# Second attention of a group as one task on four banks, with two of its minima on VectorE

## The chip, the cores and the metric

The kernel runs on one core of one Trainium2 chip. The metric is the device time of that core in microseconds (us). TensorE does the matrix products, ScalarE and VectorE empty its PSUM banks and do the elementwise work, GpSimd (POOL in the profile) does elementwise work between SBUF tiles, and SyncE starts most transfers.

## The reference

The reference is one layer of a graph attention network over 128 batches of 64 nodes with 512 features, in fp32. Cut to what matters here:

```python
def gat_heads(x, adj, W, a):                     # W: [H, F, O]
    Wh = einsum('bnf,hfo->bhno', x, W)
    e = f1(Wh)[..., None] + f2(Wh)[..., None, :]
    e = where(e > 0, e, 0.01 * e)
    e = where(adj > 0, e, -1e9)
    return einsum('bhnm,bhmo->bhno', softmax(e), Wh)

h   = relu(layernorm(x))
h   = elu(gat_heads(h, adj, W_heads, a_heads))   # first attention, 4 heads of 512
out = elu(gat_heads(concat(h), adj, W_out, a_out))  # second attention, one head of 512
y   = relu(out @ w1 + b1) @ w2 + b2 + out
return x + layernorm(y) * gamma + beta
```

The elu is `x` for positive `x` and `exp(x) - 1` otherwise.

## The kernel before

The 8192 rows are 64 tiles of 128 rows; a group is 4 tiles, and there are 16 groups. Large products of 512x512 blocks are done by a scheme of seven products instead of eight (`unit`): each of the seven is one set of 4 matmul instructions of 256 columns per weight piece, each of which the trace records as two passes, so 8 records. The seven products use three PSUM banks, and several accumulate on a bank that another engine has changed or read in between:

```python
def unit(name, product, post, order):
    own = {1: 1, 2: 1, 5: 5, 3: 5, 6: 6, 7: 6, 4: 6}      # product -> its bank
    def after(p):
        if p in (1, 5, 6):
            nm = {1: "s1", 5: "s5", 6: "t"}[p]
            sb[nm] = wk.tile([P, 2, T], FP, tag=nm, name=f"{nm}_{name}")
            if p == 6:
                nc.vector.tensor_tensor(gb[6], gb[6], sb["s1"], ALU.add)   # line 254
            nc.scalar.copy(sb[nm], gb[p])                                  # line 255
            post(nm, sb[nm])
        elif p == 2: post("c11", gb[1])
        elif p == 7: post("c22", gb[6], sb["s5"], gb[1])
        elif p == 3: post("c12", gb[5], sb["t"], gb[5])
        else:        post("c21", gb[6])
    # ... (cut: emits the parts in the given order, `after` with high priority)
```

So product 7 goes onto the bank of product 6 after the add of line 254 and the copy of line 255, and product 4 goes onto the same bank after `post("c22", ...)` has read it.

The products of the first layer run head by head in `project1` (bank names `g_a` in the trace). Each of the four results (quadrants c11, c12, c21, c22) gets an elu:

```python
def elu(dst, src, name):
    ex = wk.tile([P, 512], FP, tag="elu", name=f"ex{name}", bufs=3)
    nc.scalar.activation(ex, src, AF.Relu, scale=-1.0)                     # line 571
    nc.scalar.activation(ex, ex, AF.Exp, scale=-1.0)                       # line 572
    nc.vector.scalar_tensor_tensor(dst, ex, -1.0, src, ALU.add, ALU.max)   # line 573

# in project1, post() of a quadrant:
    if b is not None:
        nc.vector.tensor_tensor(to, a, b, ALU.add)                         # line 603 (c12, c22)
        a = to
    elu(flat(dst), flat(a), f"{what}_{g}_{h}")
# ... (cut)
    s = unit(..., (1, 5, 6, 2, 3, 7, 4))
    return [
        s[0], lambda: (s[1](), flush_late()), lambda: (s[2](), next_sums()), s[3], s[4],
        lambda: (s[5](), late.append(s[6])),
    ]
```

A head has six steps: products 1, 5, 6, 2, 3, 7. Product 4 (quadrant c21) comes late, behind product 5 of the next head; for the last head it comes behind the first part of the next stage (`project2`, bank names `g_b`).

Beside the 24 steps of the four heads run the side tasks of `stage_e`, the second attention of the group before. They are spread evenly over the steps:

```python
def attend2(g, q):
    if q == 0:
        tag = "out" if g < NG - 1 else "z11"
        OUT[g] = big.tile([P, G, FO], FP, tag=tag, name=f"o{g}")
    pa = [aux([P, FO], f"pa2_{g}_{q}_{b}") for b in range(NB)]     # aux: 2 banks
    for b in range(NB):                                            # NB = 2 batches in a tile
        rows = slice(b * N, (b + 1) * N)
        for c in range(2):
            nc.tensor.matmul(                                      # line 754, 64x64, 512 columns
                pa[b][c * N:(c + 1) * N], AT2[g][rows, 2 * q + c, rows],
                WH2[g][rows, 2 * q + c, :], start=True, stop=True, skip_group_check=True,
            )
    for b in range(NB):
        elu(OUT[g][:, 2 * q + b], pa[b], f"2_{g}_{q}_{b}")

def stage_e(g):
    gap = [lambda: None]
    score = [lambda j=j: scores2(g, j) for j in range(G)]
    attend = [lambda q=q: attend2(g, q) for q in range(2)]
    return (
        gap + score + [lambda: spread2(g)] + gap * 2 + [lambda: softmax2(g)] + gap * 5
        + [lambda: transpose_weights2(g)] + gap * 2 + attend[0:1] + gap * 2 + attend[1:2] + gap * 4
    )
```

`stage_e` runs for groups 0 to 14; the last group calls `attend2` itself, beside the feed-forward part of group 14. Of the eight PSUM banks six are the main ring ("mm", used by `bank(...)`) and two are "aux". The first attention of the first group (`attend0`, bank names `pu`) already has an elu whose minimum is taken on VectorE: `tensor_scalar(ex, pa, 0.0, None, ALU.min)` and then one Exp on ScalarE, in place of Relu and Exp.

Of the kernel before, what the change touches and what calls it, by code (L numbers as in the profile page):

```python
# [9 lines left out]
FP = mybir.dt.float32  # L10
AF = mybir.ActivationFunctionType
ALU = mybir.AluOpType
# [10 lines left out]
def gat_preln_kernel(  # L23
# [30 lines left out]
    nc = tc.nc  # L54
    P = 128
# [3 lines left out]
    FO = W_out.shape[1]  # L59
    DF = w1.shape[1]  # L60
    NB = P // N
    KC = F // P
    NT = B * N // P
    G = 4
# [9 lines left out]
    big = ctx.enter_context(tc.tile_pool(name="big", bufs=1))  # L74
# [5 lines left out]
    def bank(name):  # L80
        return ps.tile([P, 2, T], FP, tag="mm", name=name)

    def flat(ap):
        return ap.rearrange("p a b -> p (a b)")
# [8 lines left out]
    def aux(shape, name):  # L93
        return ps.tile(shape, FP, tag="aux", name=name, bufs=2)
# [470 lines left out]

    H1, ZSUM = {}, {}

    def elu(dst, src, name):

        ex = wk.tile([P, 512], FP, tag="elu", name=f"ex{name}", bufs=3)  # L570
        nc.scalar.activation(ex, src, AF.Relu, scale=-1.0)  # L571
        nc.scalar.activation(ex, ex, AF.Exp, scale=-1.0)  # L572
        nc.vector.scalar_tensor_tensor(dst, ex, -1.0, src, ALU.add, ALU.max)  # L573

    def quadrant(what):
# [12 lines left out]
    def project1(g, h):  # L588
# [8 lines left out]
        def post(what, a, b=None, to=None):  # L597
            if what[0] != "c":
                return
            nm = {"c11": "11", "c12": "12", "c21": "S1", "c22": "22"}[what]  # L600
            dst = H1[nm][:, h]
            if b is not None:
                nc.vector.tensor_tensor(to, a, b, ALU.add)  # L603
                a = to
            elu(flat(dst), flat(a), f"{what}_{g}_{h}")
            if what == "c21":
                nc.gpsimd.tensor_tensor(dst, dst, H1["22"][:, h], ALU.add)  # L607
# [96 lines left out]
    A2, AT2, F2, OUT = {}, {}, {}, {}  # L704

    def scores2(g, j):
        if j == 0:
            F2[g] = sm.tile([P, 2, G], FP, tag="f2", name=f"f2_{g}")
        f = F2[g]
        for c in range(2):  # L710
            junk = wk.tile([P, FO], FP, tag="elu", name=f"jf{g}_{j}_{c}", bufs=3)
            nc.vector.scalar_tensor_tensor(  # L712
                junk, WH2[g][:, j], 1.0, ao[:, c, :], ALU.mult, ALU.mult,
                accum_out=f[:, c, j:j + 1],
            )

    def spread2(g):

        f = F2[g]
        dg = sm.tile([P, G, N], FP, tag="s2dg", name=f"s2dg{g}", bufs=1)  # L720
        nc.vector.tensor_tensor(
            dg, eye[:, None, :].to_broadcast([P, G, N]), f[:, 1][:, :, None].to_broadcast([P, G, N]),
            ALU.mult,
        )
        F2[g] = f, dg

    def softmax2(g):
        f, dg = F2.pop(g)
        pe = aux([P, G, N], f"s2pe{g}")
        nc.tensor.matmul(  # L730
            pe.rearrange("p h m -> p (h m)"), blkones.rearrange("p b n -> p (b n)"),
            dg.rearrange("p h m -> p (h m)"), start=True, stop=True,
        )
        A2[g] = softmax(pe, f[:, 0], G, "s2", g)

    def transpose_weights2(g):
        A = A2.pop(g)
        pt = aux([P, G, P], f"s2pt{g}")
        for j in range(G):
            nc.tensor.transpose(pt[:, j, :], A[:, j].rearrange("p b m -> p (b m)"), ident)  # L740
        AT2[g] = wk.tile([P, G, P], FP, tag="hT", name=f"at2_{g}", bufs=4)
        nc.scalar.copy(AT2[g], pt)

    def attend2(g, q):


        if q == 0:
            tag = "out" if g < NG - 1 else "z11"
            OUT[g] = big.tile([P, G, FO], FP, tag=tag, name=f"o{g}")
        pa = [aux([P, FO], f"pa2_{g}_{q}_{b}") for b in range(NB)]  # L750
        for b in range(NB):
            rows = slice(b * N, (b + 1) * N)
            for c in range(2):
                nc.tensor.matmul(
                    pa[b][c * N:(c + 1) * N], AT2[g][rows, 2 * q + c, rows],
                    WH2[g][rows, 2 * q + c, :], start=True, stop=True, skip_group_check=True,
                )
        for b in range(NB):
            elu(OUT[g][:, 2 * q + b], pa[b], f"2_{g}_{q}_{b}")

    def stage_e(g):

        gap = [lambda: None]
        score = [lambda j=j: scores2(g, j) for j in range(G)]
        attend = [lambda q=q: attend2(g, q) for q in range(2)]
        return (
            gap + score + [lambda: spread2(g)] + gap * 2 + [lambda: softmax2(g)] + gap * 5
            + [lambda: transpose_weights2(g)] + gap * 2 + attend[0:1] + gap * 2 + attend[1:2] + gap * 4
        )


# [173 lines left out]
    for g in range(NG):  # L945
        if g >= 1:
            side = stage_e(g - 1)
            done, n = 0, 6 * H
            for i in range(n):
                if i % 6 == 0:  # L950
                    steps = project1(g, i // 6)
                steps[i % 6]()
                while done * n < (i + 1) * len(side):
                    side[done]()
                    done += 1
            flush_late()
# [3 lines left out]
        if g == NG - 1:  # L960
            run(project2(g), tr + [nothing] * 6 + ff[:2])
            run(ff[2:], [
                lambda: [scores2(g, j) for j in range(G)], lambda: spread2(g), nothing, nothing,
                lambda: softmax2(g), *[nothing] * 7, lambda: transpose_weights2(g), nothing,
                *[lambda q=q: attend2(g, q) for q in range(2)], nothing,
            ])
            continue
# [67 lines left out]
```

## Time and profile before

| | |
|---|---|
| time, median of 3 runs | 2297.66 us (2297.63 to 2298.43) |
| VectorE busy | 1276.5 us (56%), 2227 instructions |
| ScalarE busy | 904.6 us (39%), 1633 instructions |
| GpSimd busy | 1019.9 us (44%) |
| weight loads (PEld) busy | 1891.7 us (82%), 11856 |
| TensorE clock granted | 0.999 |
| matmuls of the second attention (`pa`, 64x512) | 256 records, median 614 ns |
| Relu from `pa` on ScalarE | 64, median 592 ns |
| Exp of these elus | 64, median 630 ns |
| last instruction of these elus on VectorE | 64, median 684 ns |

PE is TensorE's matmul and PEld its weight load, which overlaps it; DVE is VectorE, ACT is ScalarE, POOL is GpSimd, SP is SyncE. [...] matmuls that follow each other overlap in the trace, and the distance from one start to the next says more than a duration. In the second attention four matmuls on four different 64x64 parts of the array start almost together.

### The profile page before, as it was taken

The numbers are of one execution on the slowest core, as the hardware profiler recorded it, in microseconds if no ns is written. First come the engines' busy times: TensorE is split into PE (matmuls) and PEld (weight loads), VectorE is DVE, ScalarE is ACT, GpSimd is POOL, SyncE is SP. The second block draws the span as 40 slices with busy tenths as digits, with TensorE's granted clock in tenths as the row PEclk, the third lists the DMA queues.
The fourth block names the chain that finished last, engine by engine and source line by source line (L and its number), as shares of the span: only waits on it lengthen the run. The fifth ranks groups of instructions, "written<-read, shape, count | busy, mean of one in ns | idle before, by whom it ended". The sixth has DMA issues, their size and how long they took to land. (4 is left out here: it accounts for less than half of the span.)

```text
span 2293.9 us, 33254 instructions
## 1 busy us (share of the span) xinstructions
PE 2273.2 (99%) x11856; PEld 1891.7 (82%) x11856; DVE 1276.5 (56%) x2227; ACT 904.6 (39%) x1633; POOL 1019.9 (44%) x906
## 2 busy tenths in 40 slices
PE   9999999999999999999999999999999999999997
PEld 4688888888888888888888888888888888888885
DVE  7554654755556555564655546555465554644427
ACT  3535244252542525335253352534425244251512
POOL 7653524444254442634425344353443525533324
PEclk9999999999999999999999999999999999999999
DMA  8554454544546445454544645445454454635543
GB/s 288 194 183 131 147 179 133 181 132 147 174 133 184 137 156 158 136 184 130 166 151 139 183 133 176 132 147 179 133 181 133 143 177 132 183 119 169 162 147 106
DMA packets 255012, 361.15 MB, mean 157 GB/s; under 512 B 23768, under 2 KB 143608, under 8 KB 254848
## 3 DMA queue, kind: packets, MB, share of 16 engines
q1 hardware_dynamic: 249568, 340.88, 47.6%
q0 software_dynamic: 4576, 16.81, 2.0%
q8 instruction: 96, 1.57, 0.3%
q10 hardware_dynamic: 704, 1.33, 0.2%
q14 instruction: 68, 0.56, 0.1%
HBM read 331.66 MB, written 27.26 MB: 156 GB/s over the span
## 5 line engine op out<-in xcount | busy, mean ns | idle before, releaser
L305 PE MATMUL g_b<-w,h 128*128 128x256 f32 x2560 | 593.2, 380 | 0.0
L305 PEld LDWEIGHTS g_b<-w,h 128*128 128x128 f32 x2560 | 481.5, 190 | 64.1 <-issue 2.0
L289 PE MATMUL g_a<-z,w 128*128 128x256 f32 x1440 | 341.8, 380 | 0.0
L289 PE MATMUL g_a<-zs_z,w 128*128 128x256 f32 x1440 | 336.0, 381 | 0.0
L289 PEld LDWEIGHTS g_a<-zs_z,w 128*128 128x128 f32 x1440 | 270.2, 190 | 59.0 <-issue 24.4
L289 PEld LDWEIGHTS g_a<-z,w 128*128 128x128 f32 x1440 | 272.5, 190 | 41.1 <-DVE g_a L603 5.0
L305 PE MATMUL g_b<-w,hS 128*128 128x256 f32 x1024 | 238.2, 379 | 0.0
L607 POOL TENSOR_TENSOR hS<-hS,h 128x512 f32<-128x512 f32 x60 | 78.0, 1300 | 359.7 <-DVE hS L573 359.7
L305 PEld LDWEIGHTS g_b<-w,hS 128*128 128x128 f32 x1024 | 192.2, 190 | 24.8 <-issue 0.2
L571 ACT ACTIVATE exc<-g_a 128x512 f32<-128x512 f32 x240 | 142.5, 594 | 163.9 <-DVE g_a L603 95.8
L573 DVE SCALAR_TENSOR_TENSOR h<-exc,g_a 128x512 f32<-128x512 f32 x180 | 123.6, 687 | 140.7 <-ACT exc L572 140.1
L572 ACT ACTIVATE exc<-exc 128x512 f32<-128x512 f32 x240 | 151.4, 631 | 6.6
L688 POOL TENSOR_TENSOR h<-h,h 128x512 f32<-128x512 f32 x64 | 86.8, 1364 | 138.7 <-PE g_b L305 138.7
L688 POOL TENSOR_TENSOR h<-hS,h 128x512 f32<-128x512 f32 x64 | 81.7, 1277 | 146.9 <-PE g_b L305 146.7
L314 POOL TENSOR_TENSOR zs_z<-zS,z 128x512 f32<-128x512 f32 x60 | 85.2, 1419 | 134.8 <-PE g_a L289 131.6
L489 ACT COPY at<-s1pt 128x512 f32<-128x512 f32 x64 | 34.4, 589 | 268.9 <-PE s1pt L485 268.9
L833 POOL TENSOR_TENSOR xr<-xr,bs 128x512 f32<-128x512 f32 x64 | 98.8, 1546 | 78.3 <-DMA xr<-in_x_dram 45.3
L305 PE MATMUL g_d<-w,rt 128*128 128x256 f32 x512 | 121.6, 380 | 2.2 <-DVE o L825 1.5
L289 PE MATMUL g_c<-ot,w 128*128 128x256 f32 x512 | 122.7, 383 | 0.6 <-DVE ot L792 0.6
L289 PE MATMUL g_a<-zS,w 128*128 128x256 f32 x480 | 113.4, 379 | 0.0
L305 PEld LDWEIGHTS g_d<-w,rt 128*128 128x128 f32 x512 | 97.0, 190 | 16.9 <-DVE o L825 2.7
L712 DVE SCALAR_TENSOR_TENSOR jf<-wh,ao 128x512 f32<-128x512 f32 x128 | 96.7, 792 | 24.1 <-ACT wh L694 23.8
(164 smaller groups left out, 3532.9 us busy)
## 6 DMA issues: line engine op xcount, KB each, us to landing
w<-tc SPq DMA_DIRECT2D x624, 256.0 KB, 2.7
w<-in_L_gnn_W_out_dram SPq DMA_DIRECT2D x192, 256.0 KB, 2.7
w<-in_L_gnn_W_heads_dram SPq DMA_DIRECT2D x180, 256.0 KB, 3.0
w<-in_L_gnn_w_dram SPq DMA_DIRECT2D x96, 256.0 KB, 2.7
x<-in_x_dram SPq DMA_DIRECT2D x64, 256.0 KB, 4.6
xr<-in_x_dram SPq DMA_DIRECT2D x128, 128.0 KB, 2.7
out_dram<-o SPq DMA_DIRECT2D x126, 128.0 KB, 2.4
tc<-pt POOLq DMA_DIRECT2D x20, 512.0 KB, 4.3
```

What stands on the lines that cost most here:

```text
L289: LAST["pe"] = nc.tensor.matmul(bk[:, o, :], w[:, k, ts(o, P)], a[:, k, :], start=start and o == 0 and k == 0, stop=k == 1, skip_group_che ...
L305: LAST["pe"] = nc.tensor.matmul(bk[:, j, :], a[:, k, ts(j, P)], w[:, k, :], start=start and n == 0, stop=i == len(ms) - 1 and k == 1, skip ...
L314: eng.tensor_tensor(s2, s1, a11, ALU.subtract)
L489: nc.scalar.copy(AT[t].rearrange("p b h n -> p (b h) n"), pt)
L571: nc.scalar.activation(ex, src, AF.Relu, scale=-1.0)
L572: nc.scalar.activation(ex, ex, AF.Exp, scale=-1.0)
L573: nc.vector.scalar_tensor_tensor(dst, ex, -1.0, src, ALU.add, ALU.max)
L607: nc.gpsimd.tensor_tensor(dst, dst, H1["22"][:, h], ALU.add)
L688: nc.gpsimd.tensor_tensor(dst[:, h], x0[:, h], x1[:, h], ALU.subtract)
L712: nc.vector.scalar_tensor_tensor(junk, WH2[g][:, j], 1.0, ao[:, c, :], ALU.mult, ALU.mult, accum_out=f[:, c, j:j + 1],)
L833: nc.gpsimd.tensor_tensor(xr, xr, bs, ALU.add)
```

## The change

The two attention tasks of a group (`q` 0 and 1, two banks each) become one task on four banks: the two aux banks and two of the main ring. All 8 matmul instructions stand together, and the four elus follow. It stands at step 19 of 24 (counted from 0), the second step of the last head; the two tasks before stood at steps 16 and 19. In each pair of elus the second takes its minimum on VectorE, as `attend0` does. The last group keeps two tasks but has the changed elus. It is for changing TensorE's tile size once instead of twice in a group, and for taking work off ScalarE where four elus follow each other.

```diff
-    def elu(dst, src, name):
+    def elu(dst, src, name, on_vector=False):
         ex = wk.tile([P, 512], FP, tag="elu", name=f"ex{name}", bufs=3)
-        nc.scalar.activation(ex, src, AF.Relu, scale=-1.0)
-        nc.scalar.activation(ex, ex, AF.Exp, scale=-1.0)
+        if on_vector:
+            nc.vector.tensor_scalar(ex, src, 0.0, None, ALU.min)
+            nc.scalar.activation(ex, ex, AF.Exp)
+        else:
+            nc.scalar.activation(ex, src, AF.Relu, scale=-1.0)
+            nc.scalar.activation(ex, ex, AF.Exp, scale=-1.0)
         nc.vector.scalar_tensor_tensor(dst, ex, -1.0, src, ALU.add, ALU.max)
 ...
-        pa = [aux([P, FO], f"pa2_{g}_{q}_{b}") for b in range(NB)]
+        second_attention(g, q, [aux([P, FO], f"pa2_{g}_{q}_{b}") for b in range(NB)])()
+
+    def attend2_all(g):
+        OUT[g] = big.tile([P, G, FO], FP, tag="out", name=f"o{g}")
+        pa = [[aux([P, FO], f"pa2_{g}_0_{b}") for b in range(NB)]]
+        pa.append([flat(bank(f"pa2_{g}_1_{b}")) for b in range(NB)])
+        for finish in [second_attention(g, q, pa[q]) for q in range(2)]:
+            finish()
+
+    def second_attention(g, q, pa):
         for b in range(NB):
 ...   (the matmuls as before)
-        for b in range(NB):
-            elu(OUT[g][:, 2 * q + b], pa[b], f"2_{g}_{q}_{b}")
+        def finish():
+            for b in range(NB):
+                elu(OUT[g][:, 2 * q + b], pa[b], f"2_{g}_{q}_{b}", b == 1)
+        return finish
 ...
-        attend = [lambda q=q: attend2(g, q) for q in range(2)]
         return (
             gap + score + [lambda: spread2(g)] + gap * 2 + [lambda: softmax2(g)] + gap * 5
-            + [lambda: transpose_weights2(g)] + gap * 2 + attend[0:1] + gap * 2 + attend[1:2] + gap * 4
+            + [lambda: transpose_weights2(g)] + gap * 4 + [lambda: attend2_all(g)] + gap * 4
         )
```

## The prediction

> **What bounds the kernel now.** I read the page's busy shares first, then the waits of TensorE and of its weight loads, then the timeline of one group, because the shares say which engine to look at and only the other two say whether it waits.
>
> ```profile
> span 2293.9 us, 33254 instructions
> PE 2273.2 (99%) x11856; PEld 1891.7 (82%) x11856; DVE 1276.5 (56%) x2227; ACT 904.6 (39%) x1633; POOL 1019.9 (44%) x906
> ```
>
> TensorE is busy for all but 20.7 us of the span. Busy is not speed, however, so the waits come next (columns: who waited for whom, us in total, times, longest).
>
> ```profile
> PE pab L177 <- DMA ar<-in_L_gnn_a_heads_dram: 4.5, 1, 4.5
> PE g_d L305 <- DVE o L825: 1.5, 1, 1.5
> ...
> PE pa L754 <- DVE o L573: 0.2, 1, 0.2
> ```
>
> All waits of matmuls on other engines and transfers add up to about 10 us, nearly all in the first and last stages. The weight loads show something else:
>
> ```profile
> PEld g_a L289 <- issue: 24.4, 30, 0.8
> ...
> PEld pa L754 <- issue: 5.3, 16, 0.3
> PEld pa L754 <- ACT exc L572: 5.0, 15, 0.3
> ...
> PEld g_a L289 <- DVE g_a L603: 5.0, 15, 0.3
> ```
>
> In the 15 groups with a side task there are two idle stretches per attention block that no other engine ends ("issue"): 0.33 us before its first load and 0.81 us before the first load of the next product. This is the array changing between 128x128 and 64x64 tiles. One more, of 0.33 us, comes 15 times and does have a releaser: a load of g_a that waits for VectorE at line 603. The timeline of one group shows both (start, us, engine, line; the groups repeat every 140.37 us to within 0.1 us):
>
> ```profile
> 335.52 0.21 PEld L754 LDWEIGHTS pa<-wh,at 64*64 64x64 f32 x8 [0.33 <-ACT exc L572]
> ...
> 336.54 1.59 PEld L289 LDWEIGHTS g_a<-zs_z,w 128*128 128x128 f32 x8 [0.81 <-issue]
> ...
> 338.15 1.70 PEld L289 LDWEIGHTS g_a<-z,w 128*128 128x128 f32 x8
> ...
> 343.64 0.21 PEld L754 LDWEIGHTS pa<-wh,at 64*64 64x64 f32 x8 [0.33 <-issue]
> ...
> 343.75 0.60 ACT L571 ACTIVATE exc<-g_a 128x512 f32<-128x512 f32 x1 [1.14 <-PE g_a L289]
> ...
> 344.66 1.59 PEld L289 LDWEIGHTS g_a<-zs_z,w 128*128 128x128 f32 x8 [0.81 <-issue]
> ...
> 345.04 0.69 DVE L573 SCALAR_TENSOR_TENSOR hS<-exc,g_a 128x512 f32<-128x512 f32 x1 [2.98 <-ACT exc L572]
> ...
> 347.33 0.69 DVE L573 SCALAR_TENSOR_TENSOR o<-ex,pa 128x512 f32<-128x512 f32 x1 [0.46 <-ACT ex L572]
> 347.94 0.69 DVE L254 TENSOR_TENSOR g_a<-g_a,s_a 128x512 f32<-128x512 f32 x1
> 348.00 3.43 PEld L289 LDWEIGHTS g_a<-zs_z,w 128*128 128x128 f32 x16
> ...
> 348.66 0.59 ACT L255 COPY t_a<-g_a 128x512 f32<-128x512 f32 x1 [1.36 <-DVE g_a L254]
> ...
> 351.46 0.84 PEld L305 LDWEIGHTS g_b<-w,h 128*128 128x128 f32 x4
> ...
> 351.87 0.70 DVE L603 TENSOR_TENSOR g_a<-g_a,s_a 128x512 f32<-128x512 f32 x1
> ...
> 352.63 1.59 PEld L289 LDWEIGHTS g_a<-z,w 128*128 128x128 f32 x8 [0.33 <-DVE g_a L603]
> ```
>
> Regular loads follow each other at 0.215 us, so a product of 8 takes 1.725. Without the first attention the loads of 333.49 (not shown) and 338.15 would lie 2 x 1.725 = 3.45 apart; they lie 4.66 apart, so one attention block costs TensorE 1.21 us. Its eight passes of 512 columns go four at a time, that is two rounds; a round of 512 columns is 2 x 0.215 = 0.43, so 0.86 is work and about 0.36 is the change of tile size there and back.
>
> **What the Trainium skill says.** "TensorE: Matmul & The Clock Gate", The mechanism: matmuls on different tile positions run at once but start in order. The trace agrees, 8 records in 1.09 us. "TensorEngine Tiling (Array Packing)", PSUM Bottleneck: tiling speeds up TensorE but not the evacuation, so use both ScalarE and VectorE. Here the block takes 1.02 us to the next load and its two elus last until 348.02, over 3 us more. "VectorE: DVE Perf Modes", Why PSUM operands drop a tier: an fp32 operand in PSUM runs at 1x, so a min from PSUM is not cheap; the attention of the first group has such mins, 8 of 691 ns, against 592 for the Relu that they replace. "PSUM — Partial Sum Buffer", Engine vs sequencer instructions: the queues of ScalarE and VectorE are strict FIFO. The trace agrees: the add at 347.94 stood behind the elu at 347.33, which itself had waited for ScalarE. No page states what the change of tile size costs.
>
> **The change part by part.**
> (1) Two blocks become one of four banks: one change there and back is saved, 0.36 us a group. 15 groups: 5.4 us. This is the gain if nothing waits.
> (2) The list of side tasks shrinks from 25 to 24 entries over 24 steps, so scores, spread and softmax run one step (1.73 us) later. The weights were ready 6 us before their transposes (322.57 + 0.69 against 329.59), so I count 0.
> (3) The two banks that come from the main ring last held results whose elus end well before; no wait.
> (4) All four elus now stand between the elu of the third head's last quadrant (c21) and the add of line 254 of the fourth head's product 6, in both queues. Two minima move to VectorE: 32 x 691 ns there, 32 x 592 ns off ScalarE in all. What matters is the chain, as product 7 accumulates on the bank that line 254 changes and line 255 copies, and product 4 on the same bank after line 603 has read it.
>
> I work that chain out in the order in which the built program has the instructions, zero being the Relu of c21 (343.75 before). Rules taken from the trace: Relu 0.60 for the first, then 0.58, Exp 0.63, elu 0.69, min 0.69, add 0.69, copy 0.59; a waiting instruction starts 0.03 after its releaser, one that waits for nothing 0.08 to 0.1 before the end of the one ahead; a weight load starts 0.06 after VectorE.
> ScalarE: Relu c21 0 to 0.60, Exp to 1.26. VectorE: elu c21 1.29 to 1.98.
> First pair: Relu 1.16 to 1.74, Exp to 2.41; min 1.89 to 2.58, elu 2.49 to 3.17; Exp of the min 2.61 to 3.25, elu 3.28 to 3.97.
> Second pair: Relu 3.16 to 3.74, Exp to 4.40; min 3.89 to 4.58, elu 4.49 to 5.18; Exp of the min 4.61 to 5.24, elu 5.27 to 5.96.
> Then the add of line 254, 5.88 to 6.57, and the copy of line 255, 6.60 to 7.19. Before, the copy ended at 5.50 (348.66 + 0.59).
> Product 7: its first load stood at 5.97 (348.00 + 1.725), 0.47 after the copy. In the new program two more rounds, 0.86, stand before it: 6.83 if unhindered. The copy lets it go at 7.25: 0.42 late. A load that could not run ahead costs less than it is late: a product whose first load is late takes 1.61 from load to load (336.54 to 338.15) and not 1.725, which gives 0.11 back. Next load: 7.25 + 1.61 = 8.86 (before: 351.46, so 7.71).
> Product 4: unhindered at 8.86 + 0.86 = 9.72. VectorE, behind the same backlog: Relu, Exp and elu of c11 end at 7.69, 8.35 and 9.07, the add of c12 at 9.68, the add of line 603 for c22 runs 9.59 to 10.29. Load at 10.35. Before: 8.88.
> So the load of product 4 moves by 1.47 against c21, and c21 comes 1.21 earlier since the first block is gone: +0.26 us a group, 15 x 0.26 = 3.9 us. Behind product 4 nothing waits that did not: the next banks are free by then.
> (5) The last group keeps two tasks; only the minima change. There the second attention waits for the elu that empties the second bank (the elu begins 2248.82, its bank's load 2249.55). With the min on VectorE that elu ends some 0.2 us sooner; the last elu ends later, but the sums of the next product, which queue behind it, need less waiting. I estimate -0.5 us for the tail.
> Sum: 2297.66 + 3.9 - 0.5 = 2301.1 us.
>
> **The rivals.**
> A: the gain of (1) comes in full, 2297.7 - 5.4 - 0.5 = 2291.8. For it: product 7 has 0.47 us to spare, and VectorE is busy only 56%. Against it: the spare time is less than what two more elus take (the copy's end moves 1.69 in my chain, product 7 only 0.86).
> B: product 7 waits but the wait of product 4 does not grow: per group -0.36 + 0.31, so 2296.4. Against it: the load of product 4 already waits for line 603 in each group, with 0.09 us lost, so it has no slack.
> C: my chain, 2301.1.
> D: the backlog reaches further, into the evictions of the next stage, which share ScalarE and VectorE; 0.3 us more a group, 2305.6. Against it: product 4's own delay lets both engines catch up.
>
> **Range and chances.** The time is a sum of 15 equal groups, so an error of 0.1 us in the chain is 1.5 us. The chain has about 15 links of 0.01 to 0.03 us uncertainty, mostly of one sign; I allow 0.2 us a group, and B is the likeliest other outcome. Range 2296.2 to 2304.5. Even A is only 0.26% away, so over 2% either way has 1% each.
>
> **What would show it.** The timeline of a group after the change should show one attention block of 16 loads and about 1.88 us to the next load (A and C alike); the copy of line 255 ending 7.2 us after the Relu of c21; product 7's first load just behind it; a wait on ScalarE of product 7 in the waits, 15 times, of which the page before has none; and the wait of g_a for line 603 grown from 0.33 us a time to about 0.7. The group's period should be near 140.6 us. If product 7's load stands at its regular place, step (4) is wrong and A holds; if the period grows but those two waits have not, the cause lies in (2) or (3).

## Result and the profile after

The changed kernel takes 2306.38 us (2305.15 to 2307.16, 6 runs) against 2297.64 us of the kernel before: ratio 1.0038, 95% interval 1.0025 to 1.0051. It is slower by 8.7 us, within 2% but outside the predicted range, which ended at 2304.5.

The page after, its span and TensorE's row:

```profile
span 2305.4 us, 33225 instructions
PE 2276.8 (99%) x11856; PEld 1891.5 (82%) x11856; DVE 1329.8 (58%) x2259; ACT 896.6 (39%) x1601; POOL 1015.5 (44%) x906
```

TensorE's busy time grew by only 3.6 us, the span by 11.5 us between the two profiled runs; the rest is idle time. (The profiled run of before took 2295.86 us, 1.8 less than its median; where that comes from is said at the end of the experiments.) Who waited, weight loads first (columns as before), then matmuls:

```profile
PEld g_a L289 <- issue: 18.6, 30, 0.8
...
PEld g_a L289 <- DVE g_a L607: 13.9, 30, 0.6
```

```profile
PE g_a L289 <- DVE g_a L607: 3.2, 15, 0.2
```

The waits of g_a for line 607 (line 603 before) come 30 times and not 15, 13.9 us in all and not 5.0. The timeline of one group after:

```profile
344.48 0.21 PEld L768 LDWEIGHTS pa<-wh,at 64*64 64x64 f32 x8 [0.33 <-issue]
344.48 1.95 PE L768 MATMUL pa<-wh,at 64*64 64x512 f32 x16
344.59 0.60 ACT L575 ACTIVATE exc<-g_a 128x512 f32<-128x512 f32 x1 [1.14 <-PE g_a L289]
...
346.36 1.59 PEld L289 LDWEIGHTS g_a<-zs_z,w 128*128 128x128 f32 x8 [0.81 <-issue]
...
349.07 1.47 DVE L577 SCALAR_TENSOR_TENSOR o<-ex,pa 128x512 f32<-128x512 f32 x2
...
350.45 0.69 DVE L254 TENSOR_TENSOR g_a<-g_a,s_a 128x512 f32<-128x512 f32 x1
351.18 0.59 ACT L255 COPY t_a<-g_a 128x512 f32<-128x512 f32 x1 [1.36 <-DVE g_a L254]
...
351.83 1.59 PEld L289 LDWEIGHTS g_a<-zs_z,w 128*128 128x128 f32 x8 [0.43 <-issue]
...
353.45 0.84 PEld L305 LDWEIGHTS g_b<-w,h 128*128 128x128 f32 x4
...
354.17 0.69 DVE L607 TENSOR_TENSOR g_a<-g_a,s_a 128x512 f32<-128x512 f32 x1
...
354.91 0.73 PEld L289 LDWEIGHTS g_a<-z,w 128*128 128x128 f32 x4 [0.62 <-DVE g_a L607]
```

One block of 16 passes now, and the first load behind it 1.88 us later (346.36 - 344.48): that is two rounds of 0.43 more than the 1.02 of before, and only one change of tile size. Then the queue: two elus of the second pair end at 350.54, the add of line 254 runs 350.45 to 351.14, the copy of line 255 ends at 351.77, and the first load of product 7 stands at 351.83, right behind the copy. The profile names no releaser for it ("issue"), but the last load ahead of it ended at 351.40 (349.70 + 1.70), and loads that follow each other without a wait leave no such gap. The add of line 607 for c22 runs to 354.86, and product 4's first load follows at 354.91 with 0.62 us idle before it.

The groups repeat every 140.77 us, against 140.37 before (distance of the first transposes of o in successive groups, median of 11, which agree within 0.01 us). The last stage, from the last transposes of o to the end, takes 45.0 us against 41.5.

### The profile page after: what moved, and what is told of

Same layout as the page of the kernel before. It is cut to its first block, busy times and chain, and to the rows that moved or that the text cites. A ratio compares the mean times of both kernels' runs of the same rounds, so it can differ in the third digit from the quotient of the medians.

```text
span 2305.4 us, 33225 instructions
## 1 busy us (share of the span) xinstructions
PE 2276.8 (99%) x11856; PEld 1891.5 (82%) x11856; DVE 1329.8 (58%) x2259; ACT 896.6 (39%) x1601; POOL 1015.5 (44%) x906
## 4 chain that ended last, share of the span: by engine, by line
PE 91%; DVE 4%; ACT 2%; issue 1%; DMA 1%; POOL 0%; DVEq 0%; SPq 0%; POOLq 0%; ACTq 0%
PE g_b L305 32%; PE g_a L289 27%; PE g_c L289 8%; PE g_d L305 8%; PE pz L547 4%; PE hw L633 2%; PE pto L798 1%; PE pzS L547 1%; PE s1pt L485 1%; PE pth L362 1%; PE pa L768 1%; DVE ex L572 1%; ACT ex L573 1%; PE s1pe L405 1%; PE pf L372 1%
## 5 line engine op out<-in xcount | busy, mean ns | idle before, releaser
L289 PEld LDWEIGHTS g_a<-z,w 128*128 128x128 f32 x1440 | 269.9, 190 | 48.7 <-DVE g_a L607 13.9
L716 DVE SCALAR_TENSOR_TENSOR jf<-wh,ao 128x512 f32<-128x512 f32 x128 | 117.2, 951 | 7.8 <-ACT wh L698 7.6
L289 PEld LDWEIGHTS g_c<-ot,w 128*128 128x128 f32 x512 | 95.6, 191 | 20.1 <-issue 5.0
```

What stands on the lines that cost most here:

```text
L289: LAST["pe"] = nc.tensor.matmul(bk[:, o, :], w[:, k, ts(o, P)], a[:, k, :], start=start and o == 0 and k == 0, stop=k == 1, skip_group_che ...
L716: nc.vector.scalar_tensor_tensor(junk, WH2[g][:, j], 1.0, ao[:, c, :], ALU.mult, ALU.mult, accum_out=f[:, c, j:j + 1],)
```

## Experiments

Each ratio is to the kernel before as measured together with that row, so the first row is a range. The period and the last stage are read from the trace as above. In the expectations below, "the first kernel" is e1 and "the third kernel" is e3.

| kernel | time, us | ratio (95%) | period | last stage |
|---|---|---|---|---|
| before | 2297.5 to 2297.9 | 1 | 140.37 | 41.5 |
| changed | 2306.38 | 1.0038 (1.0025 to 1.0051) | 140.77 | 45.0 |
| e1 loop only | 2303.31 | 1.0025 (1.0016 to 1.0034) | 140.77 | 41.6 |
| e2 last group only | 2300.04 | 1.0010 (1.0002 to 1.0019) | 140.37 | 43.5 |
| e3 softmax at its old steps | 2300.58 | 1.0014 (1.0007 to 1.0020) | 140.59 | 41.7 |
| e4 step 17 | 2292.99 | 0.9979 (0.9970 to 0.9989) | 140.01 | 41.4 |
| e5 order in the last stage | 2303.65 | 1.0025 (1.0015 to 1.0035) | 140.78 | 41.7 |
| e6 Relu at step 19 | 2291.65 | 0.9972 (0.9961 to 0.9983) | 140.01 | 41.4 |
| e7 Relu at step 17 | 2292.82 | 0.9978 (0.9970 to 0.9987) | 140.01 | 41.4 |
| e8 step 18 | 2292.29 | 0.9977 (0.9968 to 0.9985) | 140.01 | 41.5 |
| e9 last elu behind the add | 2291.54 | 0.9972 (0.9962 to 0.9983) | 140.01 | 41.5 |
| e10 add behind the last elu | 2308.87 | 1.0048 (1.0033 to 1.0063) | 141.13 | 41.7 |

### e1 and e2: the loop and the last group apart

```diff
 # e1: the changed kernel
-                elu(..., b == 1)
+                elu(..., b == 1 and g < NG - 1)
 # e2: the kernel before, elu() with on_vector
-            elu(OUT[g][:, 2 * q + b], pa[b], f"2_{g}_{q}_{b}")
+            elu(OUT[g][:, 2 * q + b], pa[b], f"2_{g}_{q}_{b}", b == 1 and g == NG - 1)
```

> The changed kernel, but the last group's own attention keeps its old elus (no minimum on VectorE), so VectorE's order in the last stage is that of before. Theory (the loss has two parts, 15 equal groups and the last stage): the period of a group stays at 140.77 us and the last stage, from the last transposes of o to the end, goes back from 45.0 to about 41.5 us; total about 2303. Rival (the last stage is longer only because the kernel before it has drifted against its transfers): the last stage stays near 45 us and the time near 2306.

> The kernel before, with only the minima of the last group's elus on VectorE. Theory: period 140.37 us as before, last stage 45.0 us, total about 2301. Rival: last stage as before, 41.5 us, total 2297 to 2298.

e1 loses 5.8 us and e2 2.6 us, together 8.4 of the 8.7. The loop is one cause (e1 has the period of the changed kernel; 15 x 0.40 = 6.0 us), the last stage another. The size of the second is less sure: in e2 the last stage grew by 2.0 us in the profiled run, not by the 3.5 of the changed kernel that was expected.

### e3: the softmax back at its steps

```diff
-            + [lambda: transpose_weights2(g)] + gap * 4 + [lambda: attend2_all(g)] + gap * 4
+            + [lambda: transpose_weights2(g)] + gap * 5 + [lambda: attend2_all(g)] + gap * 4
```

(The list has 25 entries again; the merged task stays at step 19. The last group has its old elus here and in e4 and e6 to e10.)

> As the first kernel of this call, with one more empty entry before the merged attention, so that the list of side tasks has 25 entries again and scores, spread, softmax and transposes stand at the steps of before; the merged attention stays at step 19. Theory (the later softmax delays the add of c22 of the second head on VectorE, and product 4 waits for it): the late load of product 4 beside the third head vanishes, 0.17 us a group, period 140.59 us, total about 2300.5. Rival (that wait comes from the banks or from ScalarE): period stays at 140.77.

The period fell by 0.174 us against e1, to 140.59, as the theory had it. The wait is seen in the timeline of the changed kernel beside the third head:

```profile
328.08 0.69 DVE L460 TENSOR_TENSOR s2A<-s2e,s2rb 128x512 f32<-128x512 f32 x1
...
328.69 0.68 DVE L577 SCALAR_TENSOR_TENSOR h<-exc,g_a 128x512 f32<-128x512 f32 x1
329.29 0.69 DVE L607 TENSOR_TENSOR g_a<-g_a,s_a 128x512 f32<-128x512 f32 x1
...
330.03 1.59 PEld L289 LDWEIGHTS g_a<-z,w 128*128 128x128 f32 x8 [0.31 <-DVE g_a L607]
```

The softmax ends with s2A at 328.77, an elu and the add of line 607 for c22 of the second head queue behind it, and the add ends at 329.98. Product 4 of that head, due at 329.75 (the load ahead of it, not shown, stands at 328.02, and 328.02 + 1.725 = 329.75), loads at 330.03. In e3 these softmax steps run one step sooner, and of the 30 waits 15 are gone:

```profile
PEld g_a L289 <- DVE g_a L607: 9.3, 15, 0.6
```

The step is only half of the delay. In e3 s2A ends 4.61 us before the load of this product 4, in the changed kernel 0.98 before the place where it was due: 3.6 us later, and the step is 1.73. The rest comes from two softmax instructions that now run beside adds of GpSimd and take longer, in each of the 15 groups. The changed kernel:

```profile
322.37 1.50 POOL L611 TENSOR_TENSOR hS<-hS,h 128x512 f32<-128x512 f32 x1
322.78 1.38 DVE L435 SCALAR_TENSOR_TENSOR s2e<-s2e 128x256 f32<-128x256 f32 x1
...
326.75 1.27 POOL L316 TENSOR_TENSOR zs_z<-z,zs_z 128x512 f32<-128x512 f32 x1 [0.39 <-PE g_a L289]
326.84 1.21 DVE L453 TENSOR_TENSOR s2rb<-blkones,s2r 128x8 f32<-128x8 f32 x1
```

And e3:

```profile
320.90 0.42 DVE L435 SCALAR_TENSOR_TENSOR s2e<-s2e 128x256 f32<-128x256 f32 x1
...
323.88 0.17 DVE L453 TENSOR_TENSOR s2rb<-blkones,s2r 128x8 f32<-128x8 f32 x1
324.08 0.69 DVE L460 TENSOR_TENSOR s2A<-s2e,s2rb 128x512 f32<-128x512 f32 x1
...
329.38 1.70 PEld L289 LDWEIGHTS g_a<-z,w 128*128 128x128 f32 x8
```

The two instructions took 30 us more in all; with the 22 us of the 32 minima (0.69 each) that is nearly all of the 53.3 us by which VectorE's busy time grew.

Without the 1.04 us that line 453 took more, the add of c22 would by my estimate have ended at about 328.94 (329.98 - 1.04), 0.8 us before product 4 was due. So one step later might have cost nothing if the softmax had not come to stand beside these adds. That is not shown: e3 takes back the step and the meeting together, and in e3 the add of c22 also stands one elu further ahead in VectorE's queue.

### e4 and e8: the merged task at other steps

```diff
 # e4: step 17                                   # e8: step 18
-  gap * 4 + [lambda: attend2_all(g)] + gap * 4
+  gap * 3 + [lambda: attend2_all(g)] + gap * 6  # e8: gap * 4 + ... + gap * 5
```

> As the third kernel of this call, but the merged attention stands at step 17, behind product 7 of the third head, where products 1, 5 and 4 come before the next product that needs a sum of VectorE. Theory (the merged block by itself saves 0.36 us a group, and all of the loss is the backlog of the four elus in front of product 7 and product 4): period 140.01 us, no waits of g_a beyond those of before, total about 2292. Rival (four elus in a row cost as much wherever they stand): period 140.4 us or more, total 2298 or more.

> Minima on VectorE, 25 entries, the merged attention one step later than step 17 and one earlier than step 19: behind product 1 of the last head. Theory (what counts is the distance from the elus to the add of line 254; here one more product, 1.73 us, lies between than at step 19, and the backlog at step 19 was 0.4 us at product 7 and 0.4 us more at product 4): no waits of products 7 and 4, period 140.01 us. Rival (the elus delay whatever quadrant comes next): period 140.2 us or more.

Both periods are 140.009, which is 0.358 under the kernel before: the whole of one change of tile size there and back. The wait of g_a for line 607 is that of before (5.0 us, 15 times). So the merged block is worth what was worked out for it, and the elus cost nothing with more products between them and the add of line 254. At step 18 these are two and not one as expected: product 5 of the last head and product 4 of the third (loads at 341.69 and 343.31 in e8) lie between the block (339.81) and product 6 (345.04), which at step 19 follows the block at once. At step 17 they are three. One alone was not tried.

### e6, e7, e9, e10: minima or order

e6 and e7 take the merged task at steps 19 (list of e3) and 17 (list of e4) with Relu for all elus:

```diff
-                elu(OUT[g][:, 2 * q + b], pa[b], f"2_{g}_{q}_{b}", b == 1)
+                elu(OUT[g][:, 2 * q + b], pa[b], f"2_{g}_{q}_{b}")
```

> The merged attention at step 19 with 25 entries, all elus with Relu on ScalarE as before the change. Worked along the order of the built program, in which the add of line 254 now stands before the last elu on VectorE and not behind it: the copy of line 255 would end 6.4 us after the Relu of c21 (7.18 in the changed kernel), before the load of product 7 needs it at 6.83. Theory (what product 7 and product 4 wait for is VectorE's queue, which the two minima lengthen): both waits vanish, period 140.01 us, total about 2292. Rival (four elus in front of product 7 are too many in either form, and ScalarE with 8 instructions is slower than with 6): the period is 140.59 us or more, up to 141.2.

> As the kernel with the merged attention at step 17, but all elus with Relu on ScalarE. Theory (at step 17 there is room for either form, so where the minima are taken does not matter): period 140.01 us, total about 2292 to 2293. Rival (the minima on VectorE are needed at step 17 to relieve ScalarE): period above 140.1 us.

Both have 140.01. At step 19 the loss thus goes away with the two minima on VectorE, which were meant to relieve ScalarE. But in e6 the order of VectorE's queue changed too: there the built program has the add of line 254 in front of the last elu. e9 and e10 separate the two. In each group e9 differs from e3, and e10 from e6, by one exchange of two neighbours in VectorE's queue; the order on every other engine is the same:

```diff
 # e9: minima on VectorE as in e3; the last elu's final step is issued one step later and
+            ins = nc.vector.scalar_tensor_tensor(dst, ex, -1.0, src, ALU.add, ALU.max)
+            behind(ins, LAST["add6"], ...)   # add6: the add of line 254
 # e10: Relu as in e6
+                    if name[0] == "a" and name[-2:] == "_3":
+                        behind(ins, LAST["o"], ...)   # ins: the add of line 254; o: the last elu
```

> As the kernel with 25 entries and minima on VectorE at step 19 (period 140.59), with one instruction moved: the final step of the last of the four elus stands behind the add of line 254 on VectorE and not in front of it. The minima stay. Theory (the order in VectorE's queue is what costs, the minima only led to it): the copy of line 255 ends about 6.4 us after the Relu of c21, product 7 and product 4 wait no more than before, period 140.01 us, total about 2292. Rival (the two extra minima on VectorE cost by their own length): period 140.2 to 140.6 us.

> The reverse: as the kernel with all elus by Relu at step 19 (period 140.01), with one instruction moved: the add of line 254 stands behind the final step of the last elu. No minimum on VectorE. Theory (order): the copy of line 255 ends at about 7.6 us after the Relu of c21, product 7 waits some 0.75 us and product 4 more; worked along the order, period 141.05 us, total about 2307. Rival (without the minima there is no backlog): period 140.01 to 140.2 us.

e9 keeps the minima and has no loss (140.009); e10 has none of them and loses more than the changed kernel (141.125, expected 141.05). In e9's timeline the add of line 254 runs between the two elus of the second pair (line 578 here) and not behind both:

```profile
347.79 0.68 DVE L578 SCALAR_TENSOR_TENSOR o<-ex,pa 128x512 f32<-128x512 f32 x1
...
348.38 0.69 DVE L254 TENSOR_TENSOR g_a<-g_a,s_a 128x512 f32<-128x512 f32 x1
348.42 3.43 PEld L289 LDWEIGHTS g_a<-zs_z,w 128*128 128x128 f32 x16
...
349.11 0.59 ACT L255 COPY t_a<-g_a 128x512 f32<-128x512 f32 x1 [0.57 <-DVE g_a L254]
349.18 0.69 DVE L578 SCALAR_TENSOR_TENSOR o<-ex,pa 128x512 f32<-128x512 f32 x1
...
352.29 0.70 DVE L613 TENSOR_TENSOR g_a<-g_a,s_a 128x512 f32<-128x512 f32 x1
...
353.04 1.59 PEld L289 LDWEIGHTS g_a<-z,w 128*128 128x128 f32 x8 [0.33 <-DVE g_a L613]
```

The copy now ends at 349.70. Products 3 and 7 run on as 16 loads from 348.42, so the load of product 7 stood at 350.14, 0.44 after the copy; product 4 has the 0.33 us idle of before. In e10 product 7 waits in each of 15 groups, 0.6 us a time:

```profile
PE g_a L291 <- issue: 8.9, 15, 0.6
```

So at step 19 it is the place of one add in VectorE's queue that decides. The minima cost because the program built with them has the worse order, not by their own length.

### e5: the last stage

```diff
+            if g == NG - 2 and j == 1:
+                behind(ins, LAST["sums"], ...)   # ins: line 853 of finish(1); sums: line 316 of the last group
```

> The changed kernel, with one dependency more: in the last stage the final step of row block 1 of group 14 (line 853, which waits for a power on GpSimd) may not stand in front of the sums of the last group on VectorE. Theory (the last stage grows because that instruction came to stand between the sum of line 808 and the first of line 314, and holds the queue until GpSimd has done four adds): last stage back to 41 to 42.5 us, period unchanged at 140.77, total about 2303. Rival (it is the two minima themselves, or GpSimd sharing SBUF with VectorE): last stage stays at 43.5 to 45 us, total about 2306.

In the kernel before, this instruction (line 837 there) stood ahead of the sums and of the wait for their inputs:

```profile
2253.20 1.69 DVE L837 SCALAR_TENSOR_TENSOR o<-o,n2rs,xr 128x512 f32<-128x512 f32 x1
...
2256.02 0.67 DVE L792 TENSOR_TENSOR ot<-ot 128x512 f32<-128x512 f32 x1
...
2256.76 1.59 DVE L314 TENSOR_TENSOR zs_o<-ot,ot 128x512 f32<-128x512 f32 x1
```

VectorE and GpSimd in the last stage of the changed kernel:

```profile
2264.05 1.75 DVE L808 TENSOR_TENSOR ot<-ot 128x512 f32<-128x512 f32 x1
2267.47 1.74 DVE L853 SCALAR_TENSOR_TENSOR o<-o,n2rs,xr 128x512 f32<-128x512 f32 x1 [1.67 <-POOL n2rs L334]
2269.14 0.68 DVE L314 TENSOR_TENSOR zs_o<-ot,ot 128x512 f32<-128x512 f32 x1
...
2271.00 0.68 DVE L316 TENSOR_TENSOR zs_o<-ot,zs_o 128x512 f32<-128x512 f32 x1
```

```profile
2261.07 5.86 POOL L800 TENSOR_TENSOR o<-o,b2s 128x512 f32<-128x512 f32 x4 [1.94 <-PE pto L798]
2266.88 0.55 POOL L334 TENSOR_TENSOR n2rs<-n2ve,mhalf 128x1 f32<-128x1 f32 x1
```

The first instruction of line 853 needs the power of line 334, and GpSimd is busy with four adds of line 800 until 2266.93. VectorE stands idle for 1.67 us and then runs line 853 for 1.74, while the sums of line 314, on which the next product waits, stand behind. With the one dependency more:

```profile
2263.86 1.75 DVE L808 TENSOR_TENSOR ot<-ot 128x512 f32<-128x512 f32 x1
...
2266.20 1.08 DVE L314 TENSOR_TENSOR zs_o<-ot,ot 128x512 f32<-128x512 f32 x1
...
2268.53 1.75 DVE L316 TENSOR_TENSOR zs_o<-ot,zs_o 128x512 f32<-128x512 f32 x1
2270.20 1.40 DVE L853 SCALAR_TENSOR_TENSOR o<-o,n2rs,xr 128x512 f32<-128x512 f32 x2
```

Line 314 starts 0.59 us after line 808 ends and not 3.34, the last stage is 41.7 us, and the time 2.7 us less than the changed kernel's. The theory holds. The minima are still there, so here too it is the order that costs.

The profiled runs also differ before any changed instruction runs: the first product of hw, which waits for its weights from memory, starts at 11.30 us in the kernel before, at 12.73 in the changed one, and between these in all others. From there to the first transposes of o takes 205.68 us before and 206.13 after, close to the difference of the period. So 1.4 of the 11.5 us between the two spans is not the change. Group 13 took 140.1 to 141.7 us in kernels with a period of 140.0 to 141.1; the cause of that is open.

## Why the prediction was wrong

The direction, the mechanism in the loop and the size of its two waits were right. The sum came out at +3.4 us and the measurement at +8.7. By the prediction's own steps:

- (1) The saving of one change of tile size: 0.36 us predicted, 0.358 measured in e4, e6, e7, e8 and e9. The Trainium skill's "TensorEngine Tiling (Array Packing)", Key Properties, says that a change of tiling mode drains TensorE; the trace fits this, with the loads idle for 0.33 us ahead of a block and 0.81 behind it.
- (2) "I count 0" for the softmax one step later. This failed: 0.174 us a group (e1 against e3), 2.6 us in all. I compared only the end of the softmax with the transposes that read it. It did not delay these, but an instruction of another task behind it in VectorE's queue: the add of c22 of the second head, and with it product 4. I also took the softmax to move by the step of 1.73 us; it moved by 3.6, because two of its instructions came to stand beside GpSimd's adds.
- (3) No wait for the banks: right; the period of 140.009 in five kernels leaves no room for one.
- (4) The chain: copy ending 7.19 us after the Relu of c21, measured 7.18. Product 7 was to cost 0.31 us, measured 0.30 (its load at 351.83 is 0.405 behind its regular place, 349.70 + 1.725, and 0.11 of that comes back). Product 4 was to cost 0.32 more than before (1.49 us behind the load of g_b against 1.17), measured 0.29 (354.91 - 353.45 = 1.46). Without (2) that makes +0.23 us a group (e3) where I had 0.26: 3.4 us and not 3.9. The figures hold for the built order alone. My ground against rival A, that the spare time is less than what two more elus take, is too general: in e9 all four elus and both minima stand at the same step and cost nothing.
- (5) "-0.5 us for the tail". This failed in sign: +2.6 us (e2). I followed the elus and the load of the next product but not the order in which the finishing steps of the group before, which wait for GpSimd, now stood among the sums: line 853 of row block 1 held VectorE's queue idle for 1.67 us and busy for 1.74 (e5 takes back 2.7 us by moving it). The built program shows that order.

With (2) at 2.6 and (5) at +2.6 in place of 0 and -0.5, and 3.4 for (1) and (4) together, the sum is 8.6 us; 8.7 was measured. As (5) is uncertain by about a microsecond (2.0 to 3.5 in the traces), so close a sum is partly luck. In the loop nothing is left over: -0.36 + 0.30 + 0.29 + 0.17 is the 0.40 of the period. Of the rivals A to D none had these two terms. D, a backlog that reaches further, comes nearest in time (2305.6), but it is not what happened: behind product 4 nothing new waits.

I was also wrong in what to look for: the wait of product 7 is not booked on ScalarE but appears as an idle stretch without releaser, visible only because the load stands right behind the copy. Two small readings were wrong without bearing on the sum: half of the 0.33 us stretches ahead of a block are booked on ScalarE (line 572, 15 times), not as "issue"; and in B the loss of product 4 before is by the rule of (4) 0.20 us (0.31 late less 0.11), not 0.09.

## What to carry to other kernels

When work moves beside a busy queue, list every instruction that now stands behind it in each in-order queue, not only those that read its result, and compare each with the time when its own reader needs it. Look also at what a moved instruction will run beside: half of the softmax's delay was not the step but the adds of GpSimd that it met. Where two engines hand a result back to TensorE, the order of a single short instruction in a queue can decide more than which engine does the work: e9 and e3 differ by one exchange in VectorE's queue in each group, and by 9 us. In this kernel two products more between the merged block and the next result that TensorE waits for made the loss go away (e8 against e3), and so did the right order at the same place (e9).

## What the runs showed of the hardware

Two things were not expected. In the merged block the weights of the next round load during the round before, and rounds follow each other at 0.43 us, the first alone taking 0.48: so a round more costs its columns only.

And VectorE's instructions with two operands in SBUF took longer beside adds of GpSimd. The softmax's small product of line 453 (128x8) took 1.21 us in the changed kernel, where it started 0.09 us behind a GpSimd add of 1.27 us and ended with it (328.05 and 328.02), and 0.17 in e3, where no add ran beside it. Line 435 took 1.38 behind such an add, and 0.42 in e3, where it started 0.16 ahead of one (320.90 and 321.06). In the last stage an add (line 808 at 2264.05) took 1.75 us beside GpSimd's adds, against 0.68 for the same shape where GpSimd ran nothing (lines 314 and 316 at 2269.14 and 2271.00). The Trainium skill's "SBUF — State Buffer", Who interferes with whom, names a cause: the second SBUF input of a VectorE instruction comes through a port that GpSimd shares, and only one of them can hold it. The trace agrees in the lengths; which port is used no run here shows. In the profile this is a longer instruction and not a wait.
